# A selective-scan layer on one core: how the first chunk of layer 1 is opened, and where its decays, softplus and idle products stand in the order

## The chip, the cores and the metric

The kernel runs on one core of a Trainium2 chip. A core has five engines that each work through their own list of instructions in order: TensorE (PE in the profile, with its weight loads as PEld), VectorE (DVE), ScalarE (ACT), GpSimd (POOL) and SyncE (SP, which here only issues copies between memories). They wait for one another through semaphores. The metric is the time of one execution on the device in microseconds; the time of a version is the median over several executions.

## What is computed

Two layers over a picture of 64 x 64 places with 96 channels. Layer 0 is a state-space layer over four directions of the picture; the change does not touch it. Layer 1 normalizes its input by groups, and runs a Mamba block over the 4096 places as one sequence. Cut to what matters here:

```python
x  = x + layer0(group_norm(x))
xs, z = split(group_norm(x) @ W_in.T)              # 192 inner channels each
xc = silu(conv3(xs) + conv_b)                      # "u" in the kernel
dt, B, C = split(xc @ W_x.T)                       # 6, 16 and 16 columns
delta = softplus(dt @ W_dt.T + b_dt)               # "dt" in the kernel
h_t = exp(delta_t * A) * h_{t-1} + delta_t * B_t * xc_t    # 192 x 16 states
y_t = sum over the 16 states of h_t * C_t, + xc_t * D
out = x + (y * silu(z)) @ W_out.T
```

The recurrence over t is the heart: 192 channels times 16 states, 3072 rows of 4096 steps each.

## The kernel before

**Tiles and units.** Layer 1 is the class `Layer1` (L1280 to L1935). The sequence is cut into four chunks of 1024 steps. In a chunk, the 3072 rows are 24 tiles of 128 rows, called units: unit `s` has the pair of states `i // 3` and the group of 64 channels `i % 3`, with `i = s % 24`. Over the four chunks that is 96 units, and `run` (L1891) has one step for each, with three more at the end.

**What a unit needs.** For each unit, ScalarE takes the exponential of `dt * A` (`decay`, L1535: `dA`), something multiplies B by `w = dt * u` (`f`), VectorE scans along the 1024 steps (`tensor_tensor_scan`, L1570), GpSimd multiplies the result by C (`times_c`, L1583), and TensorE folds the rows of two states onto 64 channels and adds up over the pairs of states in PSUM (`fold`, L1603). Of each three units, two have `f` made on VectorE, from a B that TensorE has spread from 16 rows to 128 (`spread`, L1545, in the PSUM bank `f1`), and their decay lies in SBUF. The third (`on_pool`, L1523: `s % 3 == 0`, not unit 0) has `f` made on GpSimd (`pool_f`), from a B that a copy has read from memory (`load(0, s)`), and its decay is written to PSUM, into the bank `f0`, which the other two units' `f` use as well. Its decay can therefore be written only when the scan two units before it has read the bank.

**B in three parts.** `spread` works in bf16, so B is held as three bf16 parts whose sum is B to the needed exactness: part 0 is a cast of B, `less` (L1442) subtracts what has been cast so far with two products, and `part_of_b` (L1451) casts the rest; `less` and a cast come twice. Before the change all of these casts are on ScalarE.

**Softplus.** It is computed from an absolute value, two sigmoids, two squares (ScalarE, `soft_logistic` and `soft_square`, L212 to L222) and two VectorE instructions (`soft_vector`, L237). Sigmoid, Exp and Silu need different tables in ScalarE; a change of table is an instruction of its own. Afterwards `front_w` (L1493) makes `w`, and `front_dup` (L1498) issues copies that bring dt and w of each group of 64 channels into both halves of a 128-row tile, four issues for groups 0 and 1 in the later chunks, eight in pieces else.

**The order.** Every engine's order is the order of the calls in the program: the class `Ordered` (L371) chains each instruction to the one issued before it on the same engine. `start` (L1718) is the opening: it does all the front work of chunk 0 (conv product and Silu for `u`, the product `pd` for dt, B and C, softplus, copies) and a part of chunk 1's, and the first three decays. Then `run` goes through the units. In each step it takes one piece of `between` (L1828: front work of the next chunks and back work of the last one, mostly products on TensorE with one evicting instruction on ScalarE, kept in `self.late` and issued after the scan), one piece of `soft` (L1861: softplus of the next chunk and its copies), the decays for units ahead, the scan, GpSimd's work, the fold and `hold`.

**Idle products.** `hold` (L1615) issues matmuls with a weight of zeros into a bank of y that is open for adding; they change nothing and keep TensorE at work. `is_open` (L1633) tells whether such a bank is open at a step.

The lines of `run` around which the change turns:

```python
            if s % GROUPS == 0 and 0 < s < n:
                self.spread(s)
            ...
            if 0 < s and GROUPS <= s + 2 < n and not self.on_pool(s + 2):
                self.decay(s + 2)
            if self.on_pool(s + 1):
                self.decay(s + 1)
```

Of the kernel before, what the change touches and what calls it, by code (L numbers as in the profile page):

```python
# [13 lines left out]
AF = mybir.ActivationFunctionType  # L14
# [11 lines left out]
P = 128  # L26
HALF = DI - P
GRP = 3
NB = 512
NCH = L // NB  # L30
CH = 1024
NSC = L // CH
# [7 lines left out]
PAIRS, GROUPS = NS // 2, DI // HALF  # L40
# [1239 lines left out]
class Layer1:  # L1280
# [167 lines left out]
        )  # L1448
        self.nc.tensor.matmul(ps, self.k["less"][:, i, :], of["B"][:, col], start=False, stop=True)

    def part_of_b(self, i, c, hf, ps):  # L1451

        of, rows = self.chunks[c], (slice(0, B_ROWS), slice(0, 64), slice(32, 64))[i]
        self.nc.scalar.copy(of["B"][rows, self.part(hf)], ps[rows, :])

    def new_parts(self, c):
        self.at = c
# [154 lines left out]
                terms[:, self.part(hf)], start=False, stop=(n == PAIRS - 1),  # L1612
            )

    def hold(self, s):  # L1615

        c, i = divmod(s, UNIT)
        at = 3 if c == 0 else 0
        if i == at:
            n = 2  # L1620
        elif c == NSC - 1:
            n = 1 if i > 4 else 0
        else:
            n = 2 if i in (at + 12, at + 14) else 0
        open_y = [(k, g) for k, g in ((c, 2), (c, 0), (c - 1, 2)) if self.is_open(s, k, g)]
        for _ in range(n if open_y else 0):
            k, g = open_y[0]
            self.nc.tensor.matmul(
                self.chunks[k][f"y{g}"], self.k["zero"], free(self.k["within"], (1, NB)),
                start=False, stop=False,  # L1630
            )
# [86 lines left out]
    def start(self):  # L1718

        nc, of = self.nc, self.chunks[0]  # L1720
        self.at = 0
        xn = of["xn"] = self.tile("xn", [C, CH + 2], "xn")
# [38 lines left out]
        pv = [bank("f", [P, NB], f"pv{p}", f"f{p}") for p in range(2)] + [self.misc(0, [P, NB], "pv2")]  # L1761
        for p in range(3):
            do(self.product(pv[p], p, self.dt_taps(dbl)))
        pc1 = bank("y2", [P, NB], "pc1")
        do(self.product(pc1, 0, self.conv_taps(self.chunks[1]["xn"])))
        self.at = 1
        self.chunks[1]["u"] = self.tile("uz", [P, CW], "u")
        for p in range(3):
            col = self.part(p)
            nc.scalar.activation(sq[:, col], pv[p], AF.Abs, bias=self.vec(DTB, p))  # L1770
            soft_scalar(nc, self.k, sq[:, col], acc[:, col], sq[:, col])
            nc.vector.tensor_scalar(dt[:, col], pv[p], self.vec(DTB, p), 0.0, ALU.add, ALU.max)
        table(AF.Exp)
        self.load(1, 0)
        self.load(0, 3)
        self.load(1, 3)
        for p in range(3):
            col = self.part(p)
            soft_vector(nc, dt[:, col], acc[:, col], sq[:, col])
            self.front_w(0, col, nc.vector)  # L1780
            if p < 2:
                self.front_dup(0, 0, (col,), nc.sync)
                self.front_dup(0, 1, (col,), nc.scalar)
        self.front_dup(0, 2)
        self.spread(0)
        for s in range(GROUPS):
            self.decay(s)
        nc.scalar.activation(
            self.chunks[1]["u"][:, self.part(0)], pc1, AF.Identity, bias=self.vec(CB, 0)
        )  # L1790
        self.new_parts(0)
        for hf in range(2):
            self.part_of_b(0, 0, hf, pd[hf])
        for i in range(2):
            less = [bank(f"y{hf}", [B_ROWS, NB], f"less{i}_{hf}") for hf in range(2)]
            for hf in range(2):
                self.less(i, 0, hf, less[hf])
            for hf in range(2):
                self.part_of_b(i + 1, 0, hf, less[hf])
        self.first_z()  # L1800

    def first_z(self):

        nc, xn = self.nc, self.chunks[0]["xn"]
        pz = []
        for g in range(GROUPS):
            self.at = f"pz{g}"
            pz.append(self.tile(f"y{g}", [P, NB], f"y{g}"))
            for args, kw in self.z_product(pz[g], g, xn):
                nc.tensor.matmul(*args, **kw)  # L1810
        self.at = 0
        sz = self.chunks[0]["sz"] = self.tile("uz", [P, CW], "sz")

        for g in range(GROUPS):
            nc.scalar.copy(sz[:, self.part(g)], pz[g])

# [11 lines left out]
    def between(self, c):  # L1828

        more = c + 1 < NSC  # L1830
        if c == 0:
            yield from self.front_u(1, (1, 2))
        self.late = lambda: self.silus(c)
        yield
        if more:
            yield from self.front_dbl(c + 1)
            yield from self.front_v(c + 1)
        else:
            yield from self.empty(9)
# [21 lines left out]
    def soft(self, c):  # L1861

        def piece(c, col):

            nc, k = self.nc, self.k
            dt, acc, q = (self.chunks[c][n][:, col] for n in ("dt", "acc", "q"))
            nc.scalar.activation(q, dt, AF.Abs)
            yield
            yield
            soft_logistic(nc, k, q, acc, q)  # L1870
            yield
            for i in range(2):
                soft_square(nc, k, q, i)
            yield
            soft_vector(nc, dt, acc, q)
            yield
            self.front_w(c, col, nc.gpsimd)
            yield

        at = 13 if c == 0 else 10  # L1880
        for i in range(UNIT):
            if c + 1 < NSC:
                if i == at:
                    done = piece(c + 1, slice(0, CW))
                if i >= at:
                    next(done, None)
                if 0 <= i - at - 6 < GROUPS:
                    self.front_dup(c + 1, i - at - 6)
            yield

    def run(self):  # L1891
# [5 lines left out]
        for s in range(n + LAG):  # L1897
# [6 lines left out]
                self.gate(c - 1, i - first)  # L1904
            if s < n:
                next(work, None)
            if s % GROUPS == 0 and 0 < s < n:
                self.spread(s)
            if s % GROUPS == 1:
                self.load(0, s + 5)  # L1910
            if s % GROUPS == 2:
                self.load(1, s + 4)
            if 0 < s and GROUPS <= s + 2 < n and not self.on_pool(s + 2):
                self.decay(s + 2)
            if self.on_pool(s + 1):
                self.decay(s + 1)
            if s < n:
                next(soft, None)
                self.scan(s)
# [198 lines left out]
```

## Time and profile before

| what | us |
|---|---|
| median of 6 executions | 574.05 (572.27 to 576.29) |
| the profiled execution: time | 573.51 |
| the profiled execution: span from first to last instruction | 571.7 |
| VectorE busy in the span | 452.3 (79%) |
| TensorE busy in the span | 479.1 (84%) |
| GpSimd busy in the span | 350.7 (61%) |
| ScalarE busy in the span | 327.4 (57%) |
| one scan of 128 x 1024 (mean) | 2.29 in chunk 0, 2.33 to 2.35 in the others |
| one product `f` of 128 x 1024 on VectorE (mean) | 1.22 |
| one load of a table into ScalarE | 1.28 |
| layer 1: last normalization statistics | from 159.7 |
| layer 1: first scan, last scan ends | 200.46, 556.10 |

Mean granted clock of TensorE over the span: 0.889 of full speed.

How to read the lines of the profile: a line of the timeline has the start and the time in us, the engine, the source line, the operation, what it writes and reads with buffer numbers left out (`dA<-dt,A`), the shapes, how many instructions were merged, and in brackets how long the engine stood idle before it and whose end released it. Nearly all instructions carry L387, the line in `Ordered` that issues them, so that the tile names tell them apart. A line of windows has the stretch, its length, then the busy time (and number) of PE, PEld, DVE, ACT and POOL, then the granted clock of TensorE, the share of the copy engines and GB/s. Idle time of an engine that does not set the end costs nothing.

### The profile page before, as it was taken

What the parts mean: (1) busy time and instruction counts of PE and PEld (TensorE: products, weight loads), DVE (VectorE), ACT (ScalarE), POOL (GpSimd) and SP (SyncE); (2) the same over time, 40 slices, a digit from 0 to 9 for tenths busy, and PEclk for the clock granted to TensorE, in tenths of its full rate; (3) what the DMA queues carried; (4) which work ended last, traced back from release to release, by engine and by line L of the source; (5) the groups of instructions that cost most, each with busy time, mean ns of one, the idle gap of its engine ahead of it and who ended that gap; (6) DMA issues with size and microseconds to landing.
All of it is one profiled execution on the core that took longest, in us unless ns stands there. A gap on an engine that the chain in (4) does not pass through costs nothing.

```text
span 571.7 us, 4902 instructions
## 1 busy us (share of the span) xinstructions
PE 479.1 (84%) x1443; PEld 173.3 (30%) x1443; DVE 452.3 (79%) x441; ACT 327.4 (57%) x497; POOL 350.7 (61%) x203
## 2 busy tenths in 40 slices
PE   4999999987889079998758997997898866789984
PEld 4444445536733022222112222221222211212211
DVE  6896989255832566797998986989899999999991
ACT  4537993478736547768536749347669446324310
POOL 7080010013320064798897986989889898999980
PEclk9996999998998669969989869598889877899988
DMA  6102900000003951454496422695344498254301
GB/s 168 26 9 50 301 3 0 0 1 1 2 28 87 205 122 37 119 126 96 98 233 151 116 74 74 152 237 129 108 112 107 95 240 210 75 130 105 88 0 34
DMA packets 27079, 56.43 MB, mean 99 GB/s; under 512 B 11680, under 2 KB 12956, under 8 KB 26786
## 3 DMA queue, kind: packets, MB, share of 16 engines
q1 hardware_dynamic: 25122, 53.45, 38.3%
q10 hardware_dynamic: 1920, 2.57, 1.7%
q8 instruction: 13, 0.21, 0.2%
q14 instruction: 24, 0.20, 0.1%
HBM read 41.20 MB, written 2.25 MB: 76 GB/s over the span
## 4 chain that ended last, share of the span: by engine, by line
PE 42%; DVE 22%; ACT 19%; issue 5%; DMA 5%; SPq 3%; POOL 3%; DVEq 0%; POOLq 0%; ACTq 0%
DVE h L387 11%; PE y L387 10%; PE pc L387 9%; DVE f L387 4%; PE po L387 4%; ACT q L387 4%; SPq L387 3%; ACT L387 3%; PE pd L387 2%; PE pw L387 2%; DMA C<-bc_dram 2%; ACT dA L387 2%; ACT wg L387 2%; ACT f L387 2%; DVE dt L387 2%
## 5 line engine op out<-in xcount | busy, mean ns | idle before, releaser
L387 POOL TENSOR_TENSOR h<-h,C 128x1024 f32<-128x1024 f32 x96 | 229.6, 2407 | 69.5 <-DMA w<-q 38.1
L387 PE MATMUL y<-h,both 128*64 128x512 f32 x384 | 121.2, 709 | 0.1
L387 DVE TENSOR_TENSOR_SCAN h<-dA,last,f 128x1024 f32<-128x1024 f32 x48 | 112.6, 2347 | 3.2
L387 DVE TENSOR_TENSOR f<-f,w 128x1024 f32<-128x1024 f32 x65 | 79.4, 1221 | 12.9 <-DMA w<-q 5.7
L387 ACT ACTIVATE dA<-dt,A 128x1024 f32<-128x1024 f32 x65 | 74.5, 1147 | 25.3 <-DMA dt<-dt 18.2
L387 POOL TENSOR_TENSOR B<-B,w 128x1024 f32<-128x1024 f32 x31 | 73.5, 2371 | 3.6 <-DMA B<-bc_dram 3.5
L387 DVE TENSOR_TENSOR_SCAN h<-f,last,B 128x1024 f32<-128x1024 f32 x24 | 55.9, 2330 | 7.9 <-issue 3.7
L387 PE MATMUL pc<-pad,cw 96*128 96x512 f32 (+1 forms) x144 | 59.4, 572 | 1.2 <-ACT v L387 1.2
L387 ACT ACTIVATE f<-dt,A 128x1024 f32<-128x1024 f32 x31 | 34.4, 1110 | 35.4 <-DVE h L387 35.3
L387 PE MATMUL f<-parts,pick 96*128 96x512 bf16 x62 | 21.2, 428 | 34.0 <-DVE h L387 34.0
L387 PE MATMUL y<-within,zeros 128*128 128x512 f32 x78 | 47.2, 713 | 0.0
L387 PEld LDWEIGHTS y<-h,both 128*64 128x64 f32 x384 | 24.1, 150 | 65.0 <-issue 47.6
L387 DVE TENSOR_TENSOR_SCAN h<-dA,f 128x1024 f32<-128x1024 f32 x17 | 38.9, 2287 | 1.2
L387 PEld LDWEIGHTS pc<-pad,cw 96*128 96x128 f32 x144 | 28.0, 198 | 32.4 <-issue 27.0
L387 PE MATMUL pc<-xn,cw 96*64 96x512 f32 (+1 forms) x78 | 32.5, 690 | 2.7 <-ACT u L387 2.7
L387 ACT ACT_TABLE_LOAD x26 | 33.4, 1283 | 2.2 <-PEq L2108 1.7
L387 POOL TENSOR_SCALAR ln_small<-ln_small 128x4 f32<-128x4 f32 x2 | 0.5, 237 | 42.5 <-DVE ln_small L387 42.5
L387 DVE TENSOR_TENSOR_SCAN h<-f,B 128x1024 f32<-128x1024 f32 x7 | 15.9, 2272 | 12.6 <-ACT f L387 9.8
L387 PEld LDWEIGHTS y<-within,zeros 128*128 128x128 f32 x78 | 14.4, 216 | 34.8 <-issue 34.8
L387 PE MATMUL po<-sz,w_out 64*96 64x512 f32 x42 | 24.7, 699 | 0.0
L387 POOL MEMSET wda<- 128x4 f32 (+3 forms) x8 | 1.0, 120 | 38.4 <-ACT wda L387 38.4
L387 PEld LDWEIGHTS <-pick 96*128 96x128 bf16 x62 | 4.4, 99 | 59.5 <-DVE h L387 38.9
(225 smaller groups left out, 736.4 us busy)
## 6 DMA issues: line engine op xcount, KB each, us to landing
C<-bc_dram SPq DMA_DIRECT2D x64, 256.0 KB, 3.7
B<-bc_dram SPq DMA_DIRECT2D x62, 256.0 KB, 3.7
dt<-dt SPq DMA_DIRECT2D x12, 256.0 KB
w<-q SPq DMA_DIRECT2D x12, 256.0 KB, 5.9
dt<-dt SPq DMA_DIRECT2D x20, 128.0 KB, 4.9
w<-q SPq DMA_DIRECT2D x20, 128.0 KB, 4.1
wB<-rows_dram SPq DMA_DIRECT2D x1, 1472.0 KB
wC<-rows_dram SPq DMA_DIRECT2D x1, 1472.0 KB
```

What stands on the lines that cost most here:

```text
L387: ins = it(*args, **kw)
```

## The change

It has four parts.

1. **The opening (`start`).** B's six casts go to VectorE and stand before and between the parts of softplus; the products `less` follow right after the `pv` products. Softplus's vector part, `w` and the copies of group 0 are now issued within the loop over the three parts of 512 columns, each part after its scalar part. Before, all three scalar parts came first. Group 1's copies stand on ScalarE's queue after the load of Exp's table, and group 2's on SP behind the B load of unit 3. All of chunk 1's conv products (before, only the first) and chunk 0's z products come in the opening, between the first decays; `first_z` goes, and `between(0)` no longer has conv products for chunk 1, so that its later pieces come three steps earlier.
2. **The order of decays in `run`.** The decay in PSUM (for unit `s + 1`) is called before the one in SBUF (for unit `s + 2`).
3. **Softplus of the next chunk (`soft`).** It starts at step 10 in every chunk (before, 13 in chunk 0). The two squares are issued in two steps, with one empty step after them; the vector part comes at step 16 (before: 17 in chunk 0, 14 else) and the copies at 18, 19 and 20 (before: 19 to 21 in chunk 0, 16 to 18 else).
4. **Idle products (`hold`).** It is called twice in a step: ahead of the spread, and at the end. In chunks 0 to 2 two idle products stand at steps 12 and 14, and two at each of the two calls of step 0 where a bank is open. In the last chunk there is one in most steps, none in steps 11 to 16, and two more ahead of each spread outside these. In all there are 48 (before: 39).

```diff
-    def part_of_b(self, i, c, hf, ps):
+    def part_of_b(self, i, c, hf, ps, engine=None):
...
-        self.nc.scalar.copy(of["B"][rows, self.part(hf)], ps[rows, :])
+        copy = engine.tensor_copy if engine else self.nc.scalar.copy
+        copy(of["B"][rows, self.part(hf)], ps[rows, :])
...
-    def hold(self, s):
+    def hold(self, s, ahead):
 
         c, i = divmod(s, UNIT)
-        at = 3 if c == 0 else 0
-        if i == at:
+        if c == NSC - 1 and i:
+            n = 0 if 11 <= i <= 16 else 1 if not ahead else 2 if i % GROUPS == 0 else 0
+        elif i == 0:
             n = 2
-        elif c == NSC - 1:
-            n = 1 if i > 4 else 0
         else:
-            n = 2 if i in (at + 12, at + 14) else 0
-        open_y = [(k, g) for k, g in ((c, 2), (c, 0), (c - 1, 2)) if self.is_open(s, k, g)]
+            n = 0 if ahead else 2 if i in (12, 14) else 0
+        open_y = [(k, g) for k, g in ((c, 2), (c, 0), (c - 1, 2)) if self.is_open(s - ahead, k, g)]
...
-        pc1 = bank("y2", [P, NB], "pc1")
-        do(self.product(pc1, 0, self.conv_taps(self.chunks[1]["xn"])))
-        self.at = 1
-        self.chunks[1]["u"] = self.tile("uz", [P, CW], "u")
+        self.load(1, 0)
+        self.new_parts(0)
+        for hf in range(2):
+            self.part_of_b(0, 0, hf, pd[hf], nc.vector)
+        less = []
+        for i in range(2):
+            less.append([bank(f"y{hf}", [B_ROWS, NB], f"less{i}_{hf}") for hf in range(2)])
+            for hf in range(2):
+                self.less(i, 0, hf, less[i][hf])
+                if i == 0:
+                    self.part_of_b(1, 0, hf, less[0][hf], nc.vector)
+
         for p in range(3):
             col = self.part(p)
             nc.scalar.activation(sq[:, col], pv[p], AF.Abs, bias=self.vec(DTB, p))
             soft_scalar(nc, self.k, sq[:, col], acc[:, col], sq[:, col])
             nc.vector.tensor_scalar(dt[:, col], pv[p], self.vec(DTB, p), 0.0, ALU.add, ALU.max)
-        table(AF.Exp)
-        self.load(1, 0)
-        self.load(0, 3)
-        self.load(1, 3)
-        for p in range(3):
-            col = self.part(p)
             soft_vector(nc, dt[:, col], acc[:, col], sq[:, col])
             self.front_w(0, col, nc.vector)
             if p < 2:
-                self.front_dup(0, 0, (col,), nc.sync)
-                self.front_dup(0, 1, (col,), nc.scalar)
+                self.front_dup(0, 0, (col,))
+            for hf in range(2 if p == 1 else 0):
+                self.part_of_b(2, 0, hf, less[1][hf], nc.vector)
+        table(AF.Exp)
+        self.spread(0)
+        self.load(0, 3)
+        for p in range(2):
+            self.front_dup(0, 1, (self.part(p),), nc.scalar)
         self.front_dup(0, 2)
-        self.spread(0)
-        for s in range(GROUPS):
-            self.decay(s)
...
+        self.load(1, 3)
+
+        next_u = self.chunks[1]
+        self.at = 1
+        next_u["u"] = self.tile("uz", [P, CW], "u")
+        self.decay(0)
+        for p, at in enumerate((bank("y2", [P, NB], "pc0"), self.misc(1, [P, NB], "pc1"), None)):
+            at = at or bank("y2", [P, NB], "pc2")
+            do(self.product(at, p, self.conv_taps(next_u["xn"])))
+            nc.scalar.activation(
+                next_u["u"][:, self.part(p)], at, AF.Identity, bias=self.vec(CB, p)
+            )
+            if p < 2:
+                self.decay(1 + p)
+        pz = [bank(f"y{g}", [P, NB], f"pz{g}") for g in range(GROUPS)]
         for g in range(GROUPS):
...
+            do(self.z_product(pz[g], g, xn))
+        sz = of["sz"] = self.tile("uz", [P, CW], "sz")
         for g in range(GROUPS):
             nc.scalar.copy(sz[:, self.part(g)], pz[g])
...
-        if c == 0:
-            yield from self.front_u(1, (1, 2))
...
-            u = self.front_u(c + 2, (0, 1, 2) if c else (2, 0, 1))
+            u = self.front_u(c + 2)
...
-            for i in range(2):
-                soft_square(nc, k, q, i)
+            soft_square(nc, k, q, 0)
+            yield
+            soft_square(nc, k, q, 1)
+            yield
             yield
             soft_vector(nc, dt, acc, q)
             yield
             self.front_w(c, col, nc.gpsimd)
             yield
 
-        at = 13 if c == 0 else 10
+        at = 10
...
-                if 0 <= i - at - 6 < GROUPS:
-                    self.front_dup(c + 1, i - at - 6)
+                if 0 <= i - at - 8 < GROUPS:
+                    self.front_dup(c + 1, i - at - 8)
...
+            if s < n:
+                self.hold(s, 1)
             if s % GROUPS == 0 and 0 < s < n:
                 self.spread(s)
...
-            if 0 < s and GROUPS <= s + 2 < n and not self.on_pool(s + 2):
-                self.decay(s + 2)
             if self.on_pool(s + 1):
                 self.decay(s + 1)
+            if GROUPS <= s + 2 < n and not self.on_pool(s + 2):
+                self.decay(s + 2)
...
             if s < n:
-                self.hold(s)
+                self.hold(s, 0)
```

More of the change, by code (lines that the diff above doesn't have):

```diff
@@ L1781, in start @@
             if p < 2:
-                self.front_dup(0, 0, (col,), nc.sync)
-                self.front_dup(0, 1, (col,), nc.scalar)
-        self.front_dup(0, 2)
-        self.spread(0)
-        for s in range(GROUPS):
-            self.decay(s)
[L1788 to L1793, printed above, removed]
-        for i in range(2):
[L1795 to L1805, printed above, removed]
-        for g in range(GROUPS):
[L1807 to L1812, printed above, removed]
+                self.front_dup(0, 0, (col,))
[6 more added lines that the diff above has]
+            self.front_dup(0, 1, (self.part(p),), nc.scalar)
+        self.front_dup(0, 2)
+        self.load(1, 3)
[12 more added lines that the diff above has]
+        pz = [bank(f"y{g}", [P, NB], f"pz{g}") for g in range(GROUPS)]
+        for g in range(GROUPS):
+            do(self.z_product(pz[g], g, xn))
+        sz = of["sz"] = self.tile("uz", [P, CW], "sz")
         for g in range(GROUPS):
@@ L1871, in piece @@
             yield
-            for i in range(2):
-                soft_square(nc, k, q, i)
+            soft_square(nc, k, q, 0)
+            yield
+            soft_square(nc, k, q, 1)
+            yield
             yield
```

## The prediction, written before the changed kernel was run

> **What bounds the kernel now.** I read the page's busy shares first, then the windows (layer 1 begins near 160 us), then the timeline of VectorE alone from 199 us on, and only then who waited for whom there. In layer 1 the 96 units of `run` go through VectorE in order: two products and three scans for every three units, 9.4 to 9.5 us, and one triple follows the next with no idle time over long stretches. So the end is set by VectorE's stream, and what can be won is its idle time. The list of waits, cut to the stream:
>
> ```profile
> DVE h L387 <- ACT f L387: 13.3, 3, 9.8
> DVE acc L387 <- ACT q L387: 8.1, 3, 4.4
> DVE h L387 <- issue: 3.7, 2, 2.5
> DVE f L387 <- PE f L387: 4.9, 5, 1.7
> ```
>
> Each row is total, times, longest. Added up row by row from the timeline, VectorE is idle 33 us between its first scan (200.46) and its last (556.10), all behind ScalarE, TensorE or a copy. The largest piece is the opening:
>
> ```profile
> 204.26 2.02 PE L387 MATMUL y_less<-dbl,ident 96*96 96x512 f32 x2 [17.60 <-ACT parts L387]
> ...
> 211.42 0.58 ACT L387 CAST parts<-y_less 32x512 bf16<-32x512 f32 x1 [0.50 <-PE y_less L387]
> ...
> 217.45 1.14 ACT L387 ACTIVATE dA<-dt,A 128x1024 f32<-128x1024 f32 x1
> 218.49 1.11 ACT L387 ACTIVATE f<-dt,A 128x1024 f32<-128x1024 f32 x1
> 219.70 2.29 DVE L387 TENSOR_TENSOR_SCAN h<-f,B 128x1024 f32<-128x1024 f32 x1 [9.78 <-ACT f L387]
> ```
>
> The scan of unit 3 needs its decay (`f`, in PSUM). ScalarE reaches it only after B's casts, which alternate with the products `less`, after three copies of z and after another decay (`dA`) that nobody needs for 3.5 us. The other two kinds of wait:
>
> ```profile
> 306.25 1.15 ACT L387 ACTIVATE dA<-dt,A 128x1024 f32<-128x1024 f32 x1
> 307.30 1.10 ACT L387 ACTIVATE f<-dt,A 128x1024 f32<-128x1024 f32 x1
> ...
> 308.49 2.35 DVE L387 TENSOR_TENSOR_SCAN h<-f,last,B 128x1024 f32<-128x1024 f32 x1 [2.51 <-issue]
> ...
> 348.49 3.18 ACT L387 ACTIVATE q<-q,soft 128x1536 f32<-128x1536 f32 x2
> ...
> 351.70 1.76 DVE L387 SCALAR_TENSOR_TENSOR acc<-q,acc 128x1536 f32<-128x1536 f32 x1 [4.40 <-ACT q L387]
> ```
>
> The first is a decay in PSUM computed second though needed first; the wait called "issue" ends as `f` ends. The second is softplus: VectorE stands at it while ScalarE finishes two squares.
>
> **The change, part by part.** *Opening, up to the copies.* Six casts of B leave ScalarE (0.575 us each) for VectorE. No row has a cast there; the nearest, VectorE's copy of `dbl` from PSUM (118x512), took 0.692, ScalarE's own 0.575 is the other end; I take 0.69. Two casts follow the `dbl` copies (end 178.3), two wait for the first `less` pair, which TensorE can begin after the `pv` products at 180.4, so they end near 184. VectorE then does part 0 (0.75 + 0.68 + 0.69 + 0.69) until 187, part 1 until 190, two casts, part 2 until 194. Before, the three products `w` ended at 189.35, 191.41 and 193.46: 2 and 1.5 earlier, 0.5 later. The casts thus cost nothing that counts, since VectorE was idle 1.08, 2.84 and 2.84 us before the three parts; without that cover they cost 6 x 0.69 = 4.1. On the queues: SP issues group 0's copies first and the B load behind them, ScalarE issues group 1's eight copies after its table load (191), in front of the first decay. The copies are bound by bandwidth (share 1.04, 248 GB/s in 190 to 196): six tiles of 0.5 MB need some 12 us wherever they start, and each issue also waits for an older copy. So I let the last copy of group 2 land near 202 as before, and the first scan come at 199 to 200.5. ScalarE's third decay ends at 203.1, as before.
>
> The Trainium skill (VectorE: DVE Perf Modes, Specifications) speaks against this part: ScalarE lies closer to PSUM, VectorE closer to SBUF. The trace agrees in size (the same 118x512 copy 0.586 on ScalarE, 0.692 on VectorE), so the rule would charge 6 x 0.1 us, and since the engine stands idle there neither changes the sum.
>
> *Opening, from 203.1 to unit 3's decay.* The products for chunk 1's u and for z now stand on TensorE between 188 and 204, where it was idle from 186.7 to 204.3. What is left on ScalarE: last u 0.7, z's last product on TensorE 1.1 (it takes the bank that u leaves), copy 0.6, Silu's table 1.3, Silu of u 1.5, `pd` on TensorE 2.2 (beside Silu of z), `dbl` copy 0.6, cast 0.5, Exp's table 1.3, the decay 1.1: 10.9, so 214.0 in place of 219.6. Silu and the first `pd` are then done, which before came at 222.2 and 225.0. But TensorE now has `less`, the spread, skips and folds of units 0 to 2 (2.1 each) and the second `pd` in a row; placed with these rows the spread of unit 6 comes near 228, the product of unit 7 at 228.5 in place of 234.3. I take 5.8. Ends: 2 if TensorE is at half clock then (it was 0.50 from 190 to 208, which doubles pz, `pd` and `less`), 9 if the 2.77 idle before unit 6 goes too.
>
> *Softplus later.* The squares go to two steps and the vector part two steps later. Chunk 1 (which also starts three units earlier): ScalarE then ends the second square about 0.4 after VectorE wants it, 2.2 of 2.71 gained. Chunk 2: the late ScalarE (TensorE's conv product ended late, 342.1) now holds unit 39's decay: table, two sigmoids, one square, table, decay lead to 352.4, where the scan waits 3.7 from 348.7; but the 3.5 us of VectorE work that used to lie ahead comes behind it, so unit 40 starts at 358.7 in place of 361.05: 2.35. Chunk 3: 0.96, all. Sum 5.5; ends 2 (the wait moves to the decay in all three) and 8.1 (all gone). What is late next: the copies of dt and w for the next chunk, two units later in chunks 1 and 2. After chunk 0 they used to be issued from 279.96 on, the last landed at 297.1, 2 us after unit 24 began. Now every chunk issues them one unit before that point, so I count nothing; if they land late it is 2 to 4 at each boundary. B loads wait behind them on SP, no more than in chunk 0 before.
>
> *Decays in PSUM first.* Worth 1.15 (the `dA` in front) at each scan that waited for `f` with `dA` before it: 308.49, 401.57, 412.74; at 340.48 TensorE's spread is late anyway (0.86) and eats it. 3.3; ends 0 (ScalarE now waits for the bank with `dA` behind it) and 4.4.
>
> *Idle products.* 48 in place of 39, each 1.06 from start to start at full clock: 9.5 us of TensorE. Those ahead of a spread lie in TensorE's wait for the bank (2.7 at 546.62, 1.5 at 498.32, 5.7 at 295.33). Without that cover a pair costs 2.1, or 3.6 at half clock (298.21). In the last chunk a triple with five of them is 3 x 1.0 folds + 0.54 spread + 5 x 1.06 = 8.84 of 9.53 us; the triple with skips is over by 2 once. I take a loss of 1.5 there. At the very end unit 90's fold and the idle product behind it ran cold (1.87 + 1.99 for 1.08 + 1.12), 1.7 us that the closing chain carries; warmer, 0.8 is gained (ends 0 and 1.7).
>
> The Trainium skill (TensorE: Matmul & The Clock Gate, The HAM clock gate) has the clock fall after an idle window of about 3.4 us and rise after a busy one. The trace says that this is not the whole of it:
>
> ```profile
> 250.00:256.00 6.00, 6.00 (x16) 1.37 (x14) 5.86 (x4) 4.54 (x7) 6.00 (x4) 0.50 0.31 79
> 328.00:334.00 6.00, 6.00 (x13) 1.36 (x10) 5.86 (x4) 3.33 (x5) 5.39 (x4) 0.50 0.29 82
> ```
>
> TensorE (third column) is busy for all 6 us and the clock (third from the end) is 0.50. By the rule the idle products would win the cold stretches; by the row they need not, and I take no gain of clock from them but the 0.8.
>
> Sum: 5.8 + 5.5 + 3.3 + 0.8 - 1.5 = 13.9. The profiled execution took 573.51 (span 571.7), 0.5 under the median 574.05; 573.51 - 13.9 = 559.6, against the median 560.1. I forecast 560, chance 0.67, own range 553 to 565.
>
> **Rivals.** *TensorE takes over* (0.17). The windows from 221 to 268 show it busy 44.8 of 47 us; the stretch that I compress has little air, and a cold clock there or at 328 to 340 gives most of the opening and of chunk 2 back: 2 + 3 + 2 + 0 = 7, time 567. Against it: 17 us of its idle time at 187 to 204 is put to use. *It does not do what it says* (0.08). Eight copy issues and the casts stand in front of the first decay and the first part; ScalarE's chain to unit 3 is as long as it was, and only single decays are gained: 1 to 3, time 572. For it: the share 1.04 of the copies. Against it: the waits on `less` (2.11, 1.55, 0.84, 0.50) leave ScalarE for certain. *Slower* (0.08). In the last chunk the idle products ahead of spreads make TensorE the bound. At half clock the triples of units 75, 78 and 90 cost 22, 17 and 17 us for 9.53: 27, less 5 of waits that cover it, against gains of 15.4 elsewhere and 2 more lost at boundaries: +9, time 582. It decides from a granted clock under about 0.93 in that chunk (8.84 of 9.53). Against it: 1.00 from 496 to 544.
>
> **How the numbers follow.** I take the likeliest, 560. The range takes in the first rival at its middle and the bounds above: 552 to 569 (lowest: all upper ends give 23, which I do not expect together). The measurement tells about 0.5% (2.9 us) from no change. Faster by more: 0.67 + 0.17 = 0.84; within: the second, 0.08; slower: the third, 0.08.
>
> **What would show it.** Scan of unit 3 at 212 to 216 with under 8 us of idle time before it; unit 7's product near 228.5; no idle time before the vector part of softplus above 1 us; `f` ahead of `dA` and no scan waiting behind a `dA`; the last triples at 9.5 us. I am wrong if the scan of unit 3 stays after 218, if VectorE's waits for `f<-parts` (TensorE) grow over 6 us in all, or if scans after 24, 48 and 72 wait for copies.

## The result, and the profile after

| version | median us (range, runs) | against before, ratio [95%] |
|---|---|---|
| before | 572.93 (564.48 to 577.76, 84) | |
| after | 576.6 (568.52 to 585.49, 42) | 1.0043 [1.0021, 1.0065] |

The ratios here and below count only the fast runs of each version, those within 1.5% of its fastest (22 of the 42 of after), while medians and ranges are over all runs. By the ratio the change makes the kernel some 2.5 us slower, by the medians 3.7; I had forecast 560. The profiled execution took 577.84 us (span 576.1, mean granted clock 0.885), 4.3 more than the one before (573.51).

The list of waits of the changed kernel (total, times, longest):

```profile
DVE h L387 <- ACT f L387: 16.8, 7, 8.2
DVE f L387 <- PE f L387: 12.5, 9, 2.5
DVE acc L387 <- ACT q L387: 0.2, 1, 0.2
```

The wait for softplus (`acc <- q`) has fallen from 8.1 us to 0.2, and the row called "issue" (3.7) is gone. But VectorE's products now wait 12.5 us for the spread `f<-parts` of TensorE, against 4.9, and scans wait 16.8 for a decay in PSUM, as long as before (13.3, and the 3.7 called "issue", which ended with a decay too). All waits of the stream, added up row by row between the first scan and the end of the last, give 30.9 us against 33.3: most of the idle time that the change was to remove moved.

The opening, from the timeline of the changed kernel:

```profile
203.37 1.15 ACT L387 ACTIVATE dA<-dt,A 128x1024 f32<-128x1024 f32 x1 [0.96 <-DMA dt<-dt]
...
207.82 1.28 ACT L387 ACT_TABLE_LOAD   x1
209.12 1.48 ACT L387 ACTIVATE u<-u 128x1536 f32<-128x1536 f32 x1
...
210.65 3.21 PE L387 MATMUL pd<-u,w_x 128*118 128x512 f32 x4 [3.48 <-ACT u L387]
213.90 0.58 ACT L387 COPY dbl<-pd 118x512 f32<-118x512 f32 x1 [1.93 <-PE pd L387]
...
216.28 1.12 ACT L387 ACTIVATE f<-dt,A 128x1024 f32<-128x1024 f32 x1
217.48 2.29 DVE L387 TENSOR_TENSOR_SCAN h<-f,B 128x1024 f32<-128x1024 f32 x1 [8.17 <-ACT f L387]
222.32 1.23 DVE L387 TENSOR_TENSOR f<-f,w 128x1024 f32<-128x1024 f32 x1 [2.55 <-PE f L387]
```

The scan of unit 3 still waits 8.17 us for its decay, since a table load, two Silus, a slow product `pd` (3.21 us) and a second table load stand ahead of it; and the product behind it waits 2.55 for a spread, which before it did not. Layer 0 ended 1.6 us earlier in this execution than in the one before, so that against the start of layer 1 the scan is only 0.6 us earlier.

The vector part of softplus in chunk 0, with GpSimd beside it, from the timeline of the changed kernel:

```profile
268.54 2.41 POOL L387 TENSOR_TENSOR h<-h,C 128x1024 f32<-128x1024 f32 x1 [1.65 <-DVE h L387]
268.65 3.92 DVE L387 SCALAR_TENSOR_TENSOR acc<-q,acc 128x1536 f32<-128x1536 f32 x1 [0.19 <-ACT q L387]
...
270.91 3.87 POOL L387 TENSOR_TENSOR B<-B,w 128x1024 f32<-128x1024 f32 x1
...
272.60 3.80 DVE L387 SCALAR_TENSOR_TENSOR dt<-dt,acc 128x1536 f32<-128x1536 f32 x1
```

VectorE hardly waits there any more (0.19), but its two instructions take 3.92 and 3.80 us; before they took 2.66 and 1.76. An account of VectorE's stream, one profiled execution each, in us ("six" are softplus's six vector instructions of 128x1536, "stream" goes from the start of the first scan to the end of the last, "rest" is the stream less the two columns before it; the versions below the first two are those of the experiments):

| version | stream | idle | six | rest |
|---|---|---|---|---|
| before | 355.64 | 33.33 | 13.66 | 308.65 |
| after | 362.79 | 30.88 | 21.33 | 310.58 |
| before, new decay order | 358.97 | 35.97 | 12.76 | 310.24 |
| after, old decay order | 349.12 | 23.99 | 17.03 | 308.10 |
| after, old softplus | 359.38 | 36.27 | 12.42 | 310.69 |
| fastest version | 345.34 | 22.58 | 14.90 | 307.86 |
| fastest, new decay order | 349.16 | 21.91 | 17.03 | 310.22 |
| fastest, old softplus | 340.77 | 18.37 | 13.95 | 308.45 |

One execution can differ from the next: a second one of the fastest version has a stream of 341.18. From before to after the waits fall by 2.5, the six grow by 7.7 and the rest by 1.9. The stream is 7.2 longer and begins 2.1 earlier (198.37 against 200.46, of which layer 0 gave 1.6), and what follows the last scan is 0.7 shorter: about 4.4, the difference of the two executions. The whole 7.2 arises in chunk 0: 103.8 us against 94.7; the others are 1.1, 0.8 and 0.1 shorter.

### The profile page after: what moved, and what is told of

The parts are those of the page before. It is cut to its first block, busy times and chain, and to the rows that moved or that the text cites. A ratio compares the mean times of both kernels' runs of the same rounds, so it can differ in the third digit from the quotient of the medians.

```text
span 576.1 us, 4943 instructions
## 1 busy us (share of the span) xinstructions
PE 489.0 (85%) x1461; PEld 176.3 (31%) x1461; DVE 463.0 (80%) x447; ACT 323.2 (56%) x491; POOL 356.7 (62%) x203
## 5 line engine op out<-in xcount | busy, mean ns | idle before, releaser
L387 PE MATMUL y<-h,both 128*64 128x512 f32 x384 | 119.8, 707 | 0.4 <-POOL h L387 0.4
L387 DVE TENSOR_TENSOR f<-f,w 128x1024 f32<-128x1024 f32 x65 | 79.3, 1221 | 16.3 <-PE f L387 12.5
L387 POOL TENSOR_TENSOR B<-B,w 128x1024 f32<-128x1024 f32 x31 | 77.6, 2504 | 0.0
L387 ACT ACTIVATE f<-dt,A 128x1024 f32<-128x1024 f32 x31 | 34.7, 1119 | 70.7 <-DVE h L387 70.6
L387 PE MATMUL y<-within,zeros 128*128 128x512 f32 x96 | 52.3, 663 | 0.0
L387 PE MATMUL f<-parts,pick 96*128 96x512 bf16 x62 | 22.4, 449 | 28.8 <-DVE h L387 28.7
L387 PE MATMUL pc<-xn,cw 96*64 96x512 f32 (+1 forms) x66 | 29.6, 690 | 0.0
L387 PEld LDWEIGHTS y<-within,zeros 128*128 128x128 f32 x96 | 16.9, 200 | 35.0 <-issue 35.0
L387 PEld LDWEIGHTS <-pick 96*128 96x128 bf16 x62 | 4.5, 101 | 55.8 <-DVE h L387 27.8
```

Source lines behind the costliest of these rows:

```text
L387: ins = it(*args, **kw)
```

## The experiments

"After" and "before" name the two kernels. Each version was timed beside runs of before on the same chip.

**1. Undo one part at a time.** The new decay order undone:

```diff
-            if self.on_pool(s + 1):
-                self.decay(s + 1)
             if GROUPS <= s + 2 < n and not self.on_pool(s + 2):
                 self.decay(s + 2)
+            if self.on_pool(s + 1):
+                self.decay(s + 1)
```

> The changed kernel with the order of decays as before (SBUF's first). Theory: the new order saves 1.1 us at some 3 to 5 scans that wait for a decay in PSUM and costs 0.06 us at each of 32 scans (2 us), so the two cancel: within 1.5 us of the changed kernel, and the steps from one triple to the next go from 9.60 to 9.53 us. Rival (ScalarE stands in front of the PSUM bank with all behind it, idle 70.6 us in place of 35.3, and that is the loss): 4 us or more under the changed kernel.

Softplus's steps and copies as before:

```diff
-            soft_square(nc, k, q, 0)
-            yield
-            soft_square(nc, k, q, 1)
-            yield
+            for i in range(2):
+                soft_square(nc, k, q, i)
             yield
...
-        at = 10
+        at = 13 if c == 0 else 10
...
-                if 0 <= i - at - 8 < GROUPS:
-                    self.front_dup(c + 1, i - at - 8)
+                if 0 <= i - at - 6 < GROUPS:
+                    self.front_dup(c + 1, i - at - 6)
```

> The changed kernel with softplus of the next chunk in the steps of before. Theory (the two vector instructions of softplus collide with GpSimd's products, 3.9 + 3.8 us where they took 1.8 + 1.8 while GpSimd stood idle): in chunks 0 and 1 VectorE waits some 2 to 4 us for the squares again and the instructions fall back to 1.8 to 2.7 us: within 2 us of the changed kernel on either side. Rival (moving softplus gained what was forecast, 5.5 us): 4 us or more over the changed kernel.

The idle products nearly as before (one call in a step, the old counts; 37 in all, since in chunk 0 they stand at steps 0, 12 and 14, not 3, 15 and 17, and no bank is open at step 0):

```diff
-            if s < n:
-                self.hold(s, 1)
...
-                self.hold(s, 0)
+                self.hold(s)
```

> The changed kernel with 39 idle products placed as before (none ahead of spreads; one per step in the last chunk). Theory: the added ones lie in waits and the clock of the last chunk was 1.00 already: within 1 us of the changed kernel. Rival (they make TensorE late): 3 us or more under it.

The opening as before (`start`, `first_z` and `between` are those of before), and with it chunk 0's steps of softplus:

```diff
-        at = 10
+        at, dup = (13, 6) if c == 0 else (10, 8)
...
+        if c == 0:
+            yield from self.front_u(1, (1, 2))
         self.late = lambda: self.silus(c)
...
-            u = self.front_u(c + 2)
+            u = self.front_u(c + 2, (0, 1, 2) if c else (2, 0, 1))
```

> The changed kernel with the opening and chunk 0's front work and softplus as before; order of decays, softplus of chunks 1 and 2 and idle products stay changed. Theory (the loss sits in chunk 0: TensorE runs cold after the new opening, 103.8 us for 24 units in place of 94.7, and the other parts gain 1 to 2 us together): 4 to 7 us under the kernel before in the best case of the parts, at least 3 us under the changed kernel; chunk 0 back to 93 to 96 us. Rival (the loss is spread over the other parts: 0.06 us more at 32 scans and idle products): within 1 us of the changed kernel.

| undone | median us (range, runs) | ratio to before [95%] |
|---|---|---|
| decay order | 566.19 (562.46 to 571.2, 12) | 0.9895 [0.9853, 0.9936] |
| softplus | 575.44 (570.49 to 581.21, 12) | 1.0032 [0.9992, 1.0073] |
| idle products | 579.51 (577.64 to 582.83, 6) | 1.0143 [1.008, 1.0205] |
| opening | 576.28 (569.52 to 580.81, 12) | 1.0034 [0.999, 1.0078] |

One part carries a loss: without the new decay order the rest of the change gains 1%. The new softplus is worth nothing that can be told beside it, and the idle products gain (1.0143 less 1.0043: 1%; by the medians 2.9 us, 0.5%, with six runs of one version), which neither expectation had. The last row is not the worth of the opening alone: its edit also puts chunk 0's conv products back into the old order (the last line shown), and that alone is worth some 6 us (experiment 5). The waits of the version with the old order:

```profile
DVE h L387 <- ACT f L387: 15.4, 5, 9.5
DVE f L387 <- PE f L387: 4.7, 6, 1.5
```

In the old order, too, the scans wait 15.4 us for a decay (16.8 in after); the products' wait for a spread is back at 4.7, from 12.5.

**2. The order alone, on the kernel before.** The two calls of `decay` swapped, as in the change; nothing else.

> The kernel before with the new order of decays alone. Theory (what stands behind the PSUM decay on ScalarE, the other decay and the evictions of TensorE's products, comes 1.1 us later in every triple, TensorE's next product with it, and the clock falls): 4 to 9 us over the kernel before, steps of triples 9.60 us. Rival (the order costs only together with the new softplus): within 1.5 us of the kernel before.

576.07 (572.99 to 578.74, 12), ratio 1.0072 [1.0043, 1.0102]: about 4 us lost by the ratio, 3 by the medians, without any other part of the change.

**3. Unit 3's decay ahead of chunk 1's Silus.** The old order, and three empty steps in `between(0)`, so that Silu, `pd` and the two table loads stand behind unit 3's decay and spread; softplus of chunk 0 back at step 13, with its old spacing, since these steps come later.

```diff
+        if c == 0:
+            yield from self.empty(3)
         self.late = lambda: self.silus(c)
```

> The changed kernel with the old order of decays, and with three empty steps ahead of chunk 0's Silu, so that the decays and the spread of units 3 and 4 stand on ScalarE and TensorE ahead of Silu and of the first product pd of chunk 1; chunk 0's softplus in the steps of before. Theory (the new opening gains nothing at unit 3 because Silu, pd, its evictions and two tables now stand in front of its decay): the wait before the scan of unit 3 falls from 8 to 9.5 us to under 2, and the time to 556 to 562, 12 to 17 us under the kernel before. Rival (TensorE's cold clock bounds the stretch anyway): the wait moves to units 4 to 12, within 3 us of the changed kernel with the old order (566.2).

564.74 (560.12 to 568.25, 6), ratio 0.9873 [0.981, 0.9937]. ScalarE's part of its timeline:

```profile
205.93 1.15 ACT L387 ACTIVATE dA<-dt,A 128x1024 f32<-128x1024 f32 x1
206.98 1.11 ACT L387 ACTIVATE f<-dt,A 128x1024 f32<-128x1024 f32 x1
...
209.18 1.28 ACT L387 ACT_TABLE_LOAD   x1
...
216.09 0.58 ACT L387 COPY dbl<-pd 118x512 f32<-118x512 f32 x1 [2.68 <-PE pd L387]
...
219.62 1.10 ACT L387 ACTIVATE f<-dt,A 128x1024 f32<-128x1024 f32 x1
```

The decay of unit 3 (206.98) now leads the table load, and the scan waits 0.82 in place of 9.46. But 8.6 us won at one scan are 1.5 at the end by the medians (566.19 to 564.74, not clear of the spread), and the expected 556 to 562 did not come: the Silu chain now stands ahead of unit 6's decay (219.62), whose scan waits 3.16 (the profile puts it down to a copy of C, but the scan starts as that decay ends, 220.8) and the product behind it 1.25 for the spread; the scan of unit 15 waits 2.48 for its decay, and a wait of 2.65 before softplus is back.

**4. The same, with conv product 2 first in every chunk.** The change had put the products of `front_u` in the order 0, 1, 2 in chunk 0 too.

```diff
-            u = self.front_u(c + 2)
+            u = self.front_u(c + 2, (2, 0, 1))
```

> The same, with the conv products of the next but one chunk begun with the third part in every chunk (two steps of six short matmuls) in place of the first (one step of six long ones; the kernel before did this in chunk 0 alone). Theory: the wait for the decay at units 12 and 36 (2.06 and 1.84 us in the changed kernel, behind ScalarE's 5.0 us wait for the conv product) goes, 1 to 3 us under the kernel without it. Rival: it moves by a step or two, within 1 us.

558.9 (553.38 to 561.67, 6), ratio 0.977 [0.9703, 0.9838]. This is the "fastest version" of what follows. It was run again beside three others, with more rounds:

> The version that was fastest so far (the change with its decay order undone, unit 3's decay and spread ahead of chunk 1's silus, conv product 2 first in every chunk), measured again beside the three below. If its 558.9 was no chance of one batch: ratio to the kernel before 0.970 to 0.982, 556 to 562 us. If it was: 0.983 to 0.99, like the change with only its decay order undone.

559.94 (555.02 to 561.89, 6), ratio 0.9751 [0.9704, 0.9798]: some 5 us under experiment 3, more than the 1 to 3 expected.

**5. The conv order alone, on after.** The edit is the one above. It acts in chunks 0 and 1; before had this order in chunk 0 alone.

> The changed kernel with conv product 2 first in every chunk, as the kernel before had it in chunk 0; nothing else. Theory (the product of part 0 is evicted by ScalarE ahead of unit 12's decay, and ran for 5.5 us at half clock): 3 to 7 us faster than the changed kernel, 570 to 573, with the scan of unit 12 no longer 2 us late. Rival (the product that comes first is late whatever part it is; the 5.8 us that it brought to the other version came from that version's other edits): within 2 us of the changed kernel, 575 to 577.

570.7 (567.94 to 574.09, 12), ratio 0.9958 [0.9929, 0.9987]: the theory's 3 to 7 us. What it removes, from the timeline of after:

```profile
245.64 5.49 PE L387 MATMUL pc<-xn,cw 96*128 96x512 f32 x6
251.17 0.69 ACT L387 ACTIVATE u<-pc,vec 128x512 f32<-128x512 f32 x1 [5.00 <-PE pc L387]
...
251.83 1.12 ACT L387 ACTIVATE f<-dt,A 128x1024 f32<-128x1024 f32 x1
```

```profile
244.00:250.00 6.00, 6.00 (x9) 1.88 (x8) 5.79 (x4) 2.17 (x2) 6.00 (x4) 0.50 0.71 176
```

Six matmuls take 5.49 us, at a granted clock of 0.50 (the window, third from its end); ScalarE stands 5.00 us at their eviction, with the decay of unit 12 behind it; the scan then waits 2.06 and the next product 1.85. With part 2 first ScalarE waits 0.61, and unit 12 not at all. With the old decay order this product took 3.29 us though it came first, and unit 12 did not wait either: this wait needs both edits. (Conv order also gained with the old decay order, in experiment 4, where the wait that went was unit 15's.) What stands ahead of the slow product under the new order: in after ScalarE waits 0.83 us at `f` (238.05) for the bank, and the eviction of `pv`, which is issued behind, comes at 240.15; TensorE stands 0.87 us for that one bank (240.87), and the clock granted from 238 to 244 is 0.57 (0.72 in the same window with the old order, whose stream is there some 3 us further on). That these lead to the clock of 0.50 is argued, not shown. Beside the new decay order the conv order is thus a second loss: undoing either one makes the change a gain.

**6. The order on the fastest version.** The two calls of `decay` as in the change.

> The fastest version with the change's decay order put back in. Theory (in every triple the new order brings the decay in SBUF and the late evictions some 1 us later on ScalarE, so TensorE's next products come later, and it adds a wait of VectorE to every first product): slower by 4 to 10 us than the fastest version, 563 to 569. Rival 1 (the order cost time only because the opening was late, and pays once that is mended): equal or up to 3 faster, 556 to 559. Rival 2 (only the extra wait, 32 x 0.06 us): 2 slower, 561.

564.03 (562.33 to 567.18, 6), ratio 0.9846 [0.9807, 0.9884], against 0.9751 for the fastest version: 5 us by the ratios, 4 by the medians. Rival 1 (it pays once the opening is mended) has fallen. The one place of chunk 2 where the order should gain, unit 54, from the timelines of both. The fastest version:

```profile
398.21 1.15 ACT L387 ACTIVATE dA<-dt,A 128x1024 f32<-128x1024 f32 x1
399.26 1.11 ACT L387 ACTIVATE f<-dt,A 128x1024 f32<-128x1024 f32 x1
400.33 0.58 ACT L387 CAST parts<-less 64x512 bf16<-64x512 f32 x1
...
400.46 2.35 DVE L387 TENSOR_TENSOR_SCAN h<-f,last,B 128x1024 f32<-128x1024 f32 x1 [0.76 <-ACT f L387]
403.82 1.23 DVE L387 TENSOR_TENSOR f<-f,w 128x1024 f32<-128x1024 f32 x1 [1.01 <-PE f L387]
...
413.35 1.23 DVE L387 TENSOR_TENSOR f<-f,w 128x1024 f32<-128x1024 f32 x1
414.62 2.35 DVE L387 TENSOR_TENSOR_SCAN h<-dA,last,f 128x1024 f32<-128x1024 f32 x1
```

The same with the new order:

```profile
399.67 1.12 ACT L387 ACTIVATE f<-dt,A 128x1024 f32<-128x1024 f32 x1
400.72 1.14 ACT L387 ACTIVATE dA<-dt,A 128x1024 f32<-128x1024 f32 x1
401.78 0.58 ACT L387 CAST parts<-less 64x512 bf16<-64x512 f32 x1
...
401.23 2.33 DVE L387 TENSOR_TENSOR_SCAN h<-f,last,B 128x1024 f32<-128x1024 f32 x1
405.27 1.23 DVE L387 TENSOR_TENSOR f<-f,w 128x1024 f32<-128x1024 f32 x1 [1.72 <-PE f L387]
...
414.88 1.23 DVE L387 TENSOR_TENSOR f<-f,w 128x1024 f32<-128x1024 f32 x1
416.21 2.35 DVE L387 TENSOR_TENSOR_SCAN h<-dA,last,f 128x1024 f32<-128x1024 f32 x1
```

The scan no longer waits (0.76 before), but the product behind it waits 1.72 in place of 1.01; 1.77 against 1.72 in all. B's cast for the next spread stands behind both decays, whichever is first (some 2.1 us after the first of them starts, in both), so the spread is as late as ever: the wait has changed its name from ScalarE to TensorE. The last two lines of each fence show what the order costs in every triple: from the product's start to the scan's 1.27 us in the old order, 1.33 in the new one. In the trace of before, 31 of the 32 scans in this place wait for a semaphore of VectorE alone: the scan before had already waited for a later instruction of ScalarE. With the order swapped (experiment 2) their `dA` is the later one; all 32 wait for a semaphore of ScalarE, and one more instruction, which waits for VectorE's, stands ahead of each. The three scans of after in this place that still wait for VectorE alone start 1.25 after their product, the other 29 1.34. Triples without idle time take 9.53 us in the old order and 9.60 in the new one, in every profile of this study (medians of some 8 to 16 triples each, 0.01 apart). Times 31 that is 2.2 us, and the column "rest" of the account shows it: +1.6, +2.5 and +2.4 in the three pairs that differ in the order alone. In the pair of this experiment the stream grows by 3.8: the rest by 2.4, softplus's six instructions by 2.1, while the waits fall by 0.7.

**7. Softplus as before, on the fastest version.** The edit of experiment 1; it changes chunks 1 and 2, since chunk 0's steps are those of before already.

> The fastest version with softplus of chunks 2 and 3 as before (both squares in one step, vector part two steps earlier). Theory (later softplus takes away a wait and pays for it in instructions that collide with GpSimd's products, 1.8 to 3.9 us): within 2 us of the fastest version, 557 to 561, the waits for q back at some 3.5 us each and the six instructions at 13 to 14 us in all. Rival (with the decays in the old order the later softplus is worth the 3.3 us that the prediction put on chunks 2 and 3): 561 to 563.

559.83 (554.96 to 561.0, 6), ratio 0.9752 [0.9707, 0.9796]: the same as the fastest version. The wait for `q` is 6.1 us in all, against 2.8.

**8. GpSimd silent beside softplus.** After, with GpSimd's products by C of units 13, 14 and 15 and `pool_f` of unit 18 left out in chunks 0 to 2, so that these units' part of y is not computed (the fold of units 13 to 15 reads other columns of `h`, not shown).

```diff
         h = self.units[s]["h"]
+        if s // UNIT < NSC - 1 and s % UNIT in (13, 14, 15):
+            return
         self.nc.gpsimd.tensor_mul(h[:, 0:CH], h[:, SHIFT:], self.units[s - s % GROUPS]["C"])
...
         of["f"] = of["B"]
+        if s // UNIT < NSC - 1 and s % UNIT == 18:
+            return
```

> The changed kernel with GpSimd's products around the vector part of softplus left out in chunks 0 to 2 (three products with C and one with B per chunk: those units' results are not the reference's). Theory (the two instructions wait for GpSimd's products): all six take 1.73 to 1.80 us in place of 2.0 to 4.0, 10.4 to 10.8 us together in place of 21.3. Rival (something else, ScalarE or the copies, slows them): at least four of the six stay over 2.5 us.

One execution: 571.92 us. Its timeline at the same place:

```profile
271.16 1.76 DVE L387 SCALAR_TENSOR_TENSOR acc<-q,acc 128x1536 f32<-128x1536 f32 x1 [0.19 <-ACT q L387]
272.95 1.76 DVE L387 SCALAR_TENSOR_TENSOR dt<-dt,acc 128x1536 f32<-128x1536 f32 x1
```

All six instructions take 1.76 us, 10.6 in all for 21.3 in after. So the longer ones in after are a collision with GpSimd and not a longer instruction.

## Why the prediction was wrong, point by point

**The step that failed: "Decays in PSUM first", 3.3, with the ends 0 and 4.4.** I priced only the scan that waits, and let the range begin at 0, with ScalarE's wait at the bank named and counted as nothing. The runs put it at a loss of 4 to 8.5 us by the ratios (1.0072 alone; 1.0043 against 0.9895; 0.9846 against 0.9751), 3 to 10 by the medians. Three terms were missing. The gain moves to the spread, whose cast stands behind both decays (unit 54: 1.77 and 1.72). The order costs 0.07 us in each triple, for one semaphore more, 2.2 us: this is the term that all three pairs show. And whatever is called behind the decay in PSUM waits for the bank with it: ScalarE's idle time there is 70.6 us in after and 47.6 with the old order (55.8 and 35.3 on the kernel before), and I take it to reach VectorE by way of the conv product at 245.64 and the waits of units 12 and 13, which experiment 5 makes likely and does not show. I had written down the condition ("ScalarE now waits for the bank with `dA` behind it") without asking what else stood behind it, the late evictions, and who waits for those: TensorE, which shares one bank with them. That the waits for `f<-parts` pass 6 us was named as a sign that I am wrong, and they are 12.5. How the loss of the order divides in chunk 0 of after, between clock, bank and collisions, was not taken further apart: softplus's six instructions are 4.3 and 2.1 us longer under the new order in two of the three pairs and 0.9 shorter in the third, and whether the order brings that stays open.

**"Opening, from 203.1 to unit 3's decay", 5.8.** Mis-sized. I put 10.9 us on ScalarE's chain from the end of the third decay to the end of unit 3's; it took 12.9 (204.43 to 217.33): `pd` 3.21 for 2.2, at a granted clock of 0.65 (210.5 to 214), and z's last copy only at 207.22. A low clock was the condition of the lower end, 2. In this execution the third decay, which waits for copies of dt, also ended 2.9 us late, counted from the start of layer 1; in that of experiment 5, which has the same opening, it did not, and the scan of unit 3 came 3.2 us earlier than in before where here it came 0.6 earlier. Below even the lower end went the second half: the scan gained 1.6 us of idle time and the product behind it lost 2.55, so that unit 7's product came at 234.40, where 228.5 was forecast and 234.32 was before. It is what my second rival says ("ScalarE's chain to unit 3 is as long as it was"), which I gave 0.08. Experiment 3 shows which part of the chain it is: the Silus, `pd` and two table loads, which unit 3 does not need. What the new opening is worth by itself is not known. The version with the old opening (576.28), which has the old conv order in chunk 0 too, is 5.6 us slower than that of experiment 5 (570.7), which has the new opening and that order in chunks 0 and 1; but in their profiled executions chunk 0 takes 97.6 us with the old opening and 98.4 with the new one, so the difference does not show in the stretch for which I had forecast it.

**Conv order in chunk 0.** The diff takes (2, 0, 1) away there, and my sum had no term for it. Experiment 5 prices the order, with the same edit in chunk 1, at 6 us (576.6 to 570.7) beside the new decay order; of the 6.9 us by which the two profiled streams differ, 5.4 lie in chunk 0.

**"Softplus later", 5.5.** The forecast of the waits was right: 8.1 us became 0.2, and 1.84 and 1.72 of it reappeared at the decays of units 15 and 39, as I had let it for unit 39. What I had not priced is that the same instructions would be slower. In before VectorE waited first, GpSimd ran out of scans to multiply, and one of the six instructions took 3.8 us; in after five take 3.8 to 4.0. The six grow by 7.7 us, nearly all that the waits gave. The Trainium skill (SBUF — State Buffer, SBUF: two separate sides) says that a VectorE instruction with two inputs in SBUF and a GpSimd instruction that reads SBUF take turns at a shared pair of ports, each holding it for its whole length. The rows agree: GpSimd's product from 268.54 ends at 270.95, and VectorE's first instruction, begun at 268.65, ends 1.62 after that, at 272.57. GpSimd's next, begun at 270.91, ends 2.21 after that, at 274.78, and VectorE's second, begun at 272.60, again 1.62 later. With GpSimd silent (experiment 8) all six take 1.76. The trace of before had the clue, a 3.81 behind a 1.91 in chunk 2.

**"Idle products", -1.5.** The sign was wrong: undone, the kernel loses 0.5 to 1%. I took no gain of clock from them, since rows of before show a clock of 0.50 beside a busy TensorE. Two windows of the last chunk, first of after and then with the old idle products, say otherwise (third from the end is the clock):

```profile
478.00:500.00 22.00, 17.40 (x50) 4.77 (x48) 21.50 (x15) 10.87 (x14) 20.98 (x10) 0.92 0.68 160
500.00:520.00 20.00, 19.25 (x55) 5.57 (x56) 19.38 (x11) 7.25 (x7) 19.12 (x9) 1.00 0.45 111
```

```profile
478.00:500.00 22.00, 14.86 (x42) 3.81 (x38) 21.49 (x14) 10.87 (x13) 20.95 (x10) 0.77 0.62 156
500.00:520.00 20.00, 15.62 (x42) 3.73 (x42) 19.37 (x12) 6.80 (x7) 19.11 (x9) 0.91 0.43 108
```

With more idle products the clock is 0.92 and 1.00, with fewer 0.77 and 0.91 (from 478 to 556, 0.96 and 0.91), and the waits for `f<-parts` are 12.5 us in after and 19.2 there. In these windows the clock went with TensorE's busy time (17.40 and 19.25 us against 14.86 and 15.62), as the Trainium skill has it (TensorE: Matmul & The Clock Gate, The HAM clock gate), and not as in the two rows for which I had set that page aside. This is one execution of each, and it is not the whole of the gain: the last chunk takes 78.5 us against 80.6, but chunk 1, where only two products differ, 93.4 against 98.8. With the old decay order no gain shows in the last chunk: 78.6 with the old products (before) and 78.6 with the new ones. The slower rival, TensorE as the bound of the last chunk, did not come: chunk 3 takes 78.5 us, and 78.6 before.

**Right.** The casts on VectorE cost 0.63 to 0.68 us each (0.69 forecast) and nothing that counts; the first scan came 0.5 us earlier than before, counted from the start of layer 1; no scan behind 24, 48 and 72 waits for a copy; the end after the last scan is 0.7 us shorter (0.8 forecast).

The forecast was thus a sum of waits taken away. Most of these waits did shrink, and for each I failed to name the next thing in line: the spread behind the scan, GpSimd behind softplus, unit 6 behind unit 3.

## What to carry to other kernels

When two producers on one engine are swapped so that the one needed first comes first, look for what else waits behind the pair: a consumer that needs both, or an eviction that frees another engine's only bank, is not a bit earlier, or later. A swap in a loop also changes which semaphores each consumer must wait for; 0.07 us in each of 31 turns was some 2 of the 4 us that it cost on the kernel before. And a wait that is taken away may have kept two engines apart: price the instruction behind it as it runs beside the other engine, not as it ran after the wait.

## What the runs showed of the hardware

- An instruction of VectorE with two inputs in SBUF (128x1536, f32) takes 1.76 us alone and up to 3.98 beside GpSimd's products, one of which took 3.87 (its kind 2.37 in the mean of before).
- The clock was 0.50 from 244 to 250 in after, with TensorE busy for all 6 us of it. Before that stretch TensorE had worked on products with 6 input rows (`pv`); whether those rows, or the wait of 0.87 us ahead of the last of them, bring it about was not tried. In before the same products precede the 0.50 from 328 to 334, and there TensorE did not wait ahead of the last of them (327.26), so that the wait is at least not needed.
- A scan that waits for a semaphore of ScalarE besides VectorE's starts 1.31 to 1.34 us after the product ahead of it, one that waits for VectorE's alone 1.25 to 1.27 (rows without idle time).
